# Graph layers on one core: three bias additions moved from VectorE to accumulating DMAs, a doubling moved to ScalarE

## The chip, the cores and the metric

The kernel runs on one core of a Trainium2 chip. TensorE (PE in the profile) multiplies matrices into PSUM, VectorE (DVE) and ScalarE (ACT) work on the 128 partitions of SBUF and PSUM, GpSimd (POOL) and SyncE (SP) here mostly issue DMAs. The metric is the time of one execution in microseconds of the device, as the median of several runs; smaller is better.

## The reference, cut to what matters

128 graphs of 64 nodes with 512 features each pass four layers, float32 throughout. Each layer ends in `x = layernorm(x + f(x))`.

```python
def _L0_gnn_ref(x, adj, W1, b1, gamma, beta, W2, b2):
    h = relu(hypergraph_conv(x, adj, W1, b1))
    h = layer_norm(h, gamma, beta)
    y = hypergraph_conv(h, adj, W2, b2)            # ... + b2
    return y + x
def _L1_gnn_ref(x, A_shape, w, a): ...             # attention over the adjacency, no bias
def _L2_gnn_ref(batch_graph, adj, W1, b1, W2, b2, W3, b3):
    x = relu(_gcn_layer(batch_graph, adj, W1, b1))
    x = relu(_gcn_layer(x, adj, W2, b2))
    return _gcn_layer(x, adj, W3, b3)              # ... + b3
def _L3_gnn_ref(x, mask, adjacency_mat, distance_mat, W_qkv, W_out, b_out):
    ...
    return out @ W_out + b_out

x = _layernorm(x + _L0_gnn_ref(x, ...))            # x + x + ... + b2: x is doubled
x = _layernorm(x + _L1_gnn_ref(x, ...))
x = _layernorm(x + _L2_gnn_ref(x, ...))            # ... + b3
x = _layernorm(x + _L3_gnn_ref(x, ...))            # ... + b_out
```

Three rows of 512 numbers are thus added to every node: `b2` in layer 0 (where `x` counts twice), `b3` in layer 2 and `b_out` in layer 3.

## The kernel before, in words

Two graphs fill the 128 partitions (a "pair"), four pairs make a group, and there are 16 groups. A group's `x` is one tile of 128 x 4 x 512 floats (1 MB), in one of three buffers; every layer works on it in place. A large product of a group (`multiply`, L546) is cut into seven smaller ones in the manner of Strassen and Winograd, named in `ORDER`: B11, T1, T2, B21, T3, B22, T4. Each is one call of `product` (L528) and eight 128x256 matmuls for a 512x512 weight (sixteen for `w2`). They share three PSUM accumulators: `pa` takes B11, T2, T3 and T4, `pc` T1 and B22, `pb` B21. Between them the accumulators are read out: after B11, T1 and T2 by `snap` (L555), after T3 by VectorE's addition at L589, after B22 by the one at L598, after T4 by L608 or L610. A product that accumulates on in `pa` cannot begin before the read of `pa` ahead of it is over.

The left-hand operand comes from `graph_T` (L470), which multiplies a group's `x` by a graph matrix, transposed, into four PSUM tiles (two for each "duo" of pairs); ScalarE copies them to SBUF (L492). VectorE then forms the sums S1 to S4 of its quarters (`Left.sums`, L514, lines L518 to L521).

Three groups are in work at a time: `a`, in layers 0 and 1 (`first_half`); `b`, in layer 2 and the front of layer 3 (`second_half`); `t`, the rest of layer 3 of the group before that. The string `order` (L1440) lists the pieces of one step, and TensorE executes them in this order. A step begins `t.v1 a.c1 t.v b.gt ...`: products B11, T1, T2 of `v` for group `t`, then `graph_T` of layer 0 for group `a`, then the other four products of `v`, then `graph_T` of layer 2 for group `b`. In the middle steps a scheduler decides, from a cost model, the order of the instructions on the other engines; `behind(key)` only asks that an instruction stands behind a named one of its own engine.

The places of the change:

- `doubled` (L890), called in `first_half` at L789 for groups 2 to 15: VectorE forms `2 x + b2`, four instructions of 128x512, in L892. Groups 0 and 1 are doubled in the written-out start, L1515. The next to touch this `x` is `constant` (L896, line L898), VectorE as well.
- `shifted` (L745), called in `second_half` (for the middle groups at L1142): VectorE adds `gb3_bc`, four instructions at L749. The next to touch this `x` is the addition at L1172.
- the addition of `bo_bc` at L1201, one VectorE instruction of 128x2048. The next to touch this `x` is the product with `Wout` (L1233), which adds `x` at L555.

GpSimd's DMA queue carries loads of rows and columns at the start, and the stores of the sums of weights that are formed once (L280), the last of them before 361 us. After that it is empty. SyncE's queue carries the loads of weights, in the order of use, into a ring of 20 buffers of 256 KB (`wring`; L236 and L238), the loads of `x` (L153) and the stores of the result (L1243).

Of the kernel before, what the change touches and what calls it, by code (L numbers as in the profile page):

```python
# [11 lines left out]
ALU = mybir.AluOpType  # L12
AX = mybir.AxisListType

P = 128
C = 64
D = 512
DH = 1024
HEADS = 8
G = 4  # L20
# [21 lines left out]
def kernel(  # L42
# [28 lines left out]
    nc = tc.nc  # L71
    NT = x.shape[0]
    NPAIR = NT // P
    NGRP = NPAIR // G
# [56 lines left out]
    ten, vec, act = Engine(nc.tensor, PE), Engine(nc.vector, DVE), Engine(nc.scalar, ACT)  # L131
# [61 lines left out]
    def load_row(src, n, name):  # L193
        t = const.tile([P, n], FP, name=name)
        nc.gpsimd.dma_start(out=t, in_=src.partition_broadcast(P))
        return t
# [244 lines left out]
    def row2(t, c0):  # L441

        return t[:, c0 : c0 + Q].unsqueeze(1).to_broadcast([P, 2, Q])
# [57 lines left out]
    def behind(key):  # L501
        return tc.issue_after(last_add[key]) if key in last_add else nullcontext()
# [222 lines left out]
    def prepare_masks(g):  # L725
        q = g["q"]
        mj, mr = g["mj"], g["mr"]

        neg = grp.tile([P, 2, 2, C], FP, name=f"neg_{q}", tag="neg", bufs=1)
        n3 = neg.rearrange("p a g j -> p (a g) j")  # L730
        vec.tensor_mul(
            n3, mj.rearrange("p a g j -> p (a g) j"), bcast(mi[:, q * G : (q + 1) * G], G)
        )
        vec.tensor_scalar(neg, neg, BIG, BIG, ALU.mult, ALU.subtract)

        m2 = grp.tile([P, G, C], FP, name=f"m2_{q}", tag="m2", bufs=1)
        vec.tensor_mul(m2, mr, bcast(mcol[:, q * G : (q + 1) * G], G))
        adt = g["adt"]
        if LD != LA:
            vec.tensor_scalar_mul(adt, adt, LD / LA)  # L740
        vec.scalar_tensor_tensor(adt, g["atc"], LG / LA, adt, ALU.mult, ALU.add)
        vec.tensor_mul(adt, adt, m2)
        g["neg"] = neg

    def shifted(g, key):  # L745

        with behind(key):
            for p in range(G):
                vec.tensor_add(g["x"][:, p, :], g["x"][:, p, :], gb3_bc)  # L749
            prepare_masks(g)  # L750


    def first_half(g):
        q, xg = g["q"], g["x"]
# [8 lines left out]
        for n in range(2):  # L763
            for i, _ in enumerate(multiply(
                [left], (w_1[n], q),
                lambda m, k: h[m][:, :, n * D + k * Q : n * D + (k + 1) * Q],
                f"l0w1{n}_{q}",
                res=lambda m, k: row2(b1_bc, n * D + k * Q),
                stops=((2, 4), (2, 3))[n] if q == 1 else (3,),
            )):  # L770
                yield f"w1{'ab'[n]}{i + 1}"
            yield "w1" + "ab"[n]

            if n == 0:
                st = small.tile([P, G, 2, 6], FP, name=f"sth_{q}", tag="sth", bufs=2)
            with behind(f"l0w1{n}_{q}"):
                for m in range(2):
                    hn = h[m][:, :, n * D : (n + 1) * D]
                    if n == 1 and m == 1:

                        act.activation(hn[:, :, Q:], hn[:, :, Q:], AF.Relu)
                        hn = hn[:, :, :Q]
                    act.activation(hn, hn, AF.Relu)  # L783
                    for p in range(2):
                        vec.bn_stats(st[:, 2 * m + p, n, :], h[m][:, p, n * D : (n + 1) * D])
            if n == 0:
                if q > 1:
                    with behind(f"l0w10_{q}"):
                        doubled(g)  # L789
                yield "resid"  # L790
        for m in range(2):
            mv = small.tile([P, 2, 2], FP, name=f"mvh_{q}_{m}", tag="mvh")
# [97 lines left out]
    def doubled(g):  # L890
        for p in range(G):
            vec.scalar_tensor_tensor(  # L892
                g["x"][:, p, :], g["x"][:, p, :], 2.0, b2_bc, ALU.mult, ALU.add
            )
# [184 lines left out]
    def second_half(g):  # L1079
        q, xg = g["q"], g["x"]  # L1080
# [34 lines left out]
        if q == 0:  # L1115
            shifted(g, f"l2b_{q}")
# [24 lines left out]
        if not alone:  # L1141
            shifted(g, f"l0w2_{q + 1}.u2")  # L1142
        h2.sums()
        if q == NGRP - 1:
            last_add["h2s"] = newest(DVE)
            shifted(g, "h2s")
# [51 lines left out]
        for _ in multiply([left], (w_q, q), turned(qT), f"q_{q}", flipped=True, stops=(5,)):  # L1198
            yield "q1"
        with behind(f"q_{q}"):  # L1200
            vec.tensor_add(xg, xg, bo_bc.unsqueeze(1).to_broadcast([P, G, D]))  # L1201
        yield "q"
        kT = big.tile([P, KD, T], FP, name=f"kT_{q}", tag="big")
        for _ in multiply([left], (w_k, q), turned(kT), f"k_{q}", flipped=True):
# [295 lines left out]
    for n, (who, q, name) in enumerate(todo):  # L1500
# [28 lines left out]
        elif who == "rest":  # L1529
            with in_turn(SP, POOL):  # L1530
                wa_parts = load_wa()
                b2_bc = load_row(b2, D, "b2_bc")
# [6 lines left out]
                gb3_bc = load_row(gb3, D, "gb3_bc")  # L1539
                bo_bc = load_row(bout, D, "bo_bc")  # L1540
# [70 lines left out]
```

## Time and profile before

| | |
|---|---|
| median of 3 runs | 2734.22 us (2732.8 to 2735.39) |
| span of the profiled execution | 2732.1 us, granted TensorE clock 1.000 |
| PE busy | 2714.7 us, 99% of the span |
| DVE busy | 2077.8 us, 76% |
| ACT busy | 803.9 us, 29% |
| POOL busy | 38.0 us, 1%, all of it before 361 us |
| DMA moved | 405.14 MB, mean 148 GB/s |
| L892, `x<-x,b_bc` | 56 instructions, mean 691 ns |
| L749, `x<-x,gb_bc` | 64 instructions, mean 685 ns |
| L1201, `x<-x,bo_bc` | 16 instructions, mean 2287 ns |

The profile was taken in one execution, whose span stands 2.1 us under the median. A row of the timeline reads: start in us from the beginning of the span, duration in us, engine, line, operation, what it writes and reads, shape, how many instructions were merged in the row, and in brackets how long the engine sat idle before it and what ended the wait. Instructions of an engine overlap: a 128x512 addition on DVE takes 0.69 us, while the next one begins 0.60 us after it. Row L127 stands for all operations that the recording helper `Engine` issues in the written-out start and end.

### The profile page before, as it was taken

How to read it: one execution, taken by the hardware profiler on the slowest of the kernel's cores; microseconds unless marked ns; L12 is line 12 of the kernel's file. 1: busy time of each engine (PE TensorE's matmuls, PEld its weight loads, DVE VectorE, ACT ScalarE, POOL GpSimd, SP SyncE). 2: the span in 40 equal slices, each digit the busy share in tenths (PEclk: the TensorE clock that was granted, in tenths of full speed). 3: DMA queues.
4: the chain of work that ended last, by engine and by line, in shares of the span. 5: the costliest groups of instructions: out<-in, count | busy, mean ns of one | idle time of the engine just before them, and what ended most of it. 6: DMA issues, size and time to landing. Idle time of an engine off the chain costs nothing.

```text
span 2732.1 us, 67726 instructions
## 1 busy us (share of the span) xinstructions
PE 2714.7 (99%) x28770; PEld 2347.7 (86%) x28770; DVE 2077.8 (76%) x4111; ACT 803.9 (29%) x1440; POOL 38.0 (1%) x71
## 2 busy tenths in 40 slices
PE   9999999999999999999999999999999999999998
PEld 7888888888888888888888888888888888888887
DVE  6878687876877778777786877778677687776766
ACT  3323223232232332323223233232322323233232
POOL 2000000000000000000000000000000000000000
PEclk9999999999999999999999999999999999999999
DMA  7545454454544545455454554545545455454541
GB/s 257 179 129 154 123 175 140 142 162 131 173 131 139 168 129 170 130 145 168 134 165 129 146 165 133 164 129 151 163 130 167 130 154 157 128 166 129 158 125 63
DMA packets 309532, 405.14 MB, mean 148 GB/s; under 512 B 57424, under 2 KB 185456, under 8 KB 309232
## 3 DMA queue, kind: packets, MB, share of 16 engines
q1 hardware_dynamic: 304256, 385.45, 48.2%
q0 software_dynamic: 4832, 15.24, 1.5%
q8 instruction: 228, 3.74, 0.6%
q14 instruction: 72, 0.59, 0.1%
q10 hardware_dynamic: 144, 0.13, 0.0%
HBM read 369.78 MB, written 30.93 MB: 147 GB/s over the span
## 4 chain that ended last, share of the span: by engine, by line
PE 96%; DVE 3%; ACT 1%; issue 0%; DMA 0%; DVEq 0%
PE a_l0w L539 15%; PE b_l0w L539 7%; PE a_l2b L539 4%; PE a_q L539 4%; PE a_k L539 4%; PE a_l2a L539 4%; PE a_v L539 4%; PE c_l0w L539 4%; PE a_l1w L539 4%; PE a_wo L539 4%; PE a_l2c L539 4%; PE gt_l L481 3%; PE gt_l0h L481 2%; PE b_l2a L539 2%; PE b_l1w L539 2%; PE b_l2b L539 2%
## 5 line engine op out<-in xcount | busy, mean ns | idle before, releaser
L539 PE MATMUL a_l0w<-w2w,aT_l0h 128*128 128x256 f32 x720 | 164.3, 381 | 0.0
L457 DVE BATCH_NORM_STATS2 st_l<-x 128x6 f32<-128x512 f32 x244 | 157.9, 676 | 0.6
L539 PEld LDWEIGHTS a_l0w<-w2w,aT_l0h 128*128 128x128 f32 x720 | 135.6, 190 | 18.8
L463 DVE TENSOR_SCALAR x<-x,mv_l,rs_l 128x512 f32<-128x512 f32 x244 | 119.3, 543 | 2.2
L539 PE MATMUL b_l0w<-w2w,s_l0h 128*128 128x256 f32 x480 | 108.5, 379 | 0.0
L783 ACT ACTIVATE h<-h 128x1024 f32<-128x1024 f32 (+1 forms) x58 | 55.0, 948 | 178.5 <-DVE h L598 157.4
L539 PEld LDWEIGHTS b_l0w<-w2w,s_l0h 128*128 128x128 f32 x480 | 91.1, 190 | 12.5
L1140 ACT ACTIVATE aT_h<-gth,gb_col 128x256 f32<-128x256 f32 x124 | 47.2, 491 | 159.0 <-PE gth L1128 159.0
L447 ACT ACTIVATE rs_l<-mv_l,eps_t 128x4 f32<-128x4 f32 (+1 forms) x63 | 18.8, 298 | 252.3 <-DVE mv_l L458 245.0
L492 ACT COPY aT_l<-gt_l 128x512 f32<-128x512 f32 x148 | 78.1, 597 | 46.4 <-PE gt_l L481 46.4
L555 DVE TENSOR_TENSOR u_l0w<-a_l0w,b_bc 128x512 f32<-128x512 f32 x56 | 38.6, 689 | 69.2 <-PE a_l0w L539 69.2
L539 PE MATMUL a_l2b<-gwbw,aT_h 128*128 128x256 f32 x360 | 86.6, 383 | 0.0
L539 PE MATMUL a_l2c<-gwcw,aT_h 128*128 128x256 f32 x360 | 86.3, 382 | 0.0
L539 PE MATMUL a_q<-aT_xT,wqw 128*128 128x256 f32 x360 | 85.1, 379 | 0.5 <-ACT aT_xT L1194 0.5
L539 PE MATMUL a_l1w<-ww,aT_l 128*128 128x256 f32 x360 | 85.1, 379 | 0.2 <-ACT aT_l L492 0.2
L539 PE MATMUL a_l2a<-aT_l,gwaw 128*128 128x256 f32 x360 | 85.0, 379 | 0.0
L539 PE MATMUL a_k<-aT_xT,wkw 128*128 128x256 f32 x360 | 85.0, 379 | 0.0
L539 PE MATMUL a_v<-wvw,aT_xT 128*128 128x256 f32 x336 | 81.1, 384 | 0.5 <-issue 0.5
L539 PE MATMUL a_l0w<-w1aw,aT_l 128*128 128x256 f32 x336 | 80.8, 383 | 0.0
L539 PE MATMUL a_wo<-wow,aT_oT 128*128 128x256 f32 x336 | 79.5, 379 | 0.0
L539 PE MATMUL a_l0w<-w1bw,aT_l 128*128 128x256 f32 x336 | 79.4, 379 | 0.0
L539 PEld LDWEIGHTS a_l2c<-gwcw,aT_h 128*128 128x128 f32 x360 | 67.2, 190 | 11.6 <-ACT u_l2c L555 3.0
(532 smaller groups left out, 6489.0 us busy)
## 6 DMA issues: line engine op xcount, KB each, us to landing
w2w<-w2k SPq DMA_DIRECT2D x210, 256.0 KB, 2.7
x<-in_x_dram SPq DMA_DIRECT2D x15, 1024.0 KB, 5.8
w1aw<-w1ak SPq DMA_DIRECT2D x60, 256.0 KB, 2.7
w1bw<-w1bk SPq DMA_DIRECT2D x60, 256.0 KB, 2.8
ww<-wk SPq DMA_DIRECT2D x60, 256.0 KB, 2.7
gwaw<-gwak SPq DMA_DIRECT2D x60, 256.0 KB, 3.4
gwbw<-gwbk SPq DMA_DIRECT2D x60, 256.0 KB, 2.7
gwcw<-gwck SPq DMA_DIRECT2D x60, 256.0 KB, 2.7
```

The source lines that it names most:

```text
L447: act.activation(rs[:, at], mv[:, at, 1], AF.Sqrt, bias=eps_t)
L457: vec.bn_stats(st, xg[:, p, :])
L463: vec.tensor_scalar(xg[:, p, :], xg[:, p, :], mv[:, p, 0:1], rs[:, p : p + 1], ALU.subtract, ALU.mult)
L481: ten.matmul(ps[g][f * C : (f + 1) * C, c, p, :], src(2 * duo + p)[rows, c0 : c0 + C], mat[rows, 2 * duo + p, :], start=True, stop=True,)
L492: act.copy(o[:, :, :, g, :], ps[g])
L539: ten.matmul(acc[:, blk, :], lhsT, rhs, start=(first and blk == 0 and i == 0), stop=(last and i == n_k - 1), skip_group_check=True,)
L555: last_add[f"{key}.{what}"] = (act.copy(t, ps) if res is None else vec.tensor_add(t, ps, res(m, n))).ins
L783: act.activation(hn, hn, AF.Relu)
L1140: act.activation(o[:, :, h, :], cols, AF.Relu, bias=gb2_col[:, k : k + 1])
```

## The change

A function `add_rows` issues one DMA on GpSimd's queue that adds a row of 512 floats, repeated over partitions and pairs, to a whole `x` tile of 1 MB in SBUF, by accumulation. It takes the place of VectorE's additions of `gb3_bc` and `bo_bc` in groups 1 to 14. In `first_half`, for groups 2 to 15, ScalarE multiplies the four pairs of `x` by 2.0, and `add_rows` adds `b2_bc`. Groups 0, 1 and 15 keep the old way where the diff says so. In all 42 DMAs and 56 multiplications are added, and 56 instructions of L892, 56 of L749 and 14 of L1201 are removed.

```diff
+    def add_rows(xg, row):
+
+        nc.gpsimd.dma_start(out=xg, in_=row.unsqueeze(1).to_broadcast([P, G, D]), accum_op=ALU.add)
+
     def shifted(g, key):
 
         with behind(key):
-            for p in range(G):
-                vec.tensor_add(g["x"][:, p, :], g["x"][:, p, :], gb3_bc)
+            if 0 < g["q"] < NGRP - 1:
+                add_rows(g["x"], gb3_bc)
+            else:
+                for p in range(G):
+                    vec.tensor_add(g["x"][:, p, :], g["x"][:, p, :], gb3_bc)
             prepare_masks(g)
...
             if n == 0:
                 if q > 1:
                     with behind(f"l0w10_{q}"):
-                        doubled(g)
+                        for p in range(G):
+                            act.mul(xg[:, p, :], xg[:, p, :], 2.0)
+                        add_rows(xg, b2_bc)
                 yield "resid"
...
         with behind(f"q_{q}"):
-            vec.tensor_add(xg, xg, bo_bc.unsqueeze(1).to_broadcast([P, G, D]))
+            if 0 < q < NGRP - 1:
+                add_rows(xg, bo_bc)
+            else:
+                vec.tensor_add(xg, xg, bo_bc.unsqueeze(1).to_broadcast([P, G, D]))
         yield "q"
```

The compiled program of the changed kernel has the same instructions in the same order on TensorE. On ScalarE the multiplications stand, in each of the 14 steps, where `graph_T` of layer 0 is copied out; at the same place VectorE's order differs too. Line numbers are those of the kernel before, "new" marks the added instructions.

```
ScalarE before              ScalarE after               VectorE before        VectorE after
L555 u_v<-a_v               L555 u_v<-a_v               L518 S1<-aT_l         L518 S1<-aT_l
L492 aT_l<-gt_l             new  x<-x (pair 0)          L519 S2               L568 v<-c_v,u_v
L492 aT_l<-gt_l             L492 aT_l<-gt_l             L520 S3               L519 S2
L492 aT_l<-gt_l             L492 aT_l<-gt_l             L521 S4               L520 S3
L492 aT_l<-gt_l             new  x<-x (pair 1)          L568 v<-c_v,u_v       L521 S4
L608 v<-a_v                 new  x<-x (pair 2)          L589 v<-a_v,u_v       L589 v<-a_v,u_v
                            L492 aT_l<-gt_l             L598 v<-b_v,u_v       L598 v<-b_v,u_v
                            L492 aT_l<-gt_l
                            new  x<-x (pair 3)
                            L608 v<-a_v
```

Two more exchanges recur in each step on ScalarE: the exponential of the last softmax quarter (L1337) moves ahead of the second `relu` of L783, and the square root for layer 3's normalization (L447) moves from behind two of the copies `u_k<-a_k`, `u_k<-b_k` (L555) to ahead of both. The number of ScalarE's table loads stays the same. On GpSimd's queue a step issues the DMA of `b2` for group `a`, then of `gb3` and of `bo` for group `b`.

## The prediction

> **What bounds the kernel now.** I read the page's busy times first, then the chain of waits by engine, then busy time by stretches of one step each, which decide.
>
> ```profile
> PE 2714.7 (99%) x28770; PEld 2347.7 (86%) x28770; DVE 2077.8 (76%) x4111; ACT 803.9 (29%) x1440; POOL 38.0 (1%) x71
> ...
> PE 96%; DVE 3%; ACT 1%; issue 0%; DMA 0%; DVEq 0%
> ```
>
> ```profile
> 1155.69:1323.67 167.98, 167.98 (x1793) 145.53 (x1793) 128.78 (x254) 49.37 (x89) 0.00 (x0) 1.00 0.51 148
> 1323.67:1491.63 167.96, 167.96 (x1793) 145.59 (x1793) 128.79 (x254) 49.36 (x89) 0.00 (x0) 1.00 0.50 148
> ...
> 1827.57:1996.97 169.40, 168.13 (x1794) 145.59 (x1793) 128.87 (x254) 49.57 (x89) 0.00 (x0) 1.00 0.51 147
> 1996.97:2164.94 167.97, 167.97 (x1793) 145.59 (x1793) 128.78 (x254) 49.37 (x89) 0.00 (x0) 1.00 0.51 148
> ```
>
> Each row is a step, cut at the first `w2` matmul of two groups in succession: length, then busy time of PE, PEld, DVE, ACT and POOL, the granted clock, the DMA engines' share, GB/s. A step takes 167.96 to 167.98 us and PE is busy for all of it, at clock 1.00. The one longer step holds a pause of 1.27 us that ended with "issue", in which PE waited for nothing that the profile names. So steps run at the pace of back-to-back matmuls (216 ns from one to the next). PE's idle time in the whole span is 2732.1 - 2714.7 = 17.4 us, of which 9.6 us are pauses before 202 us or behind 2638 us, outside the 14 changed steps. DVE is idle for 39 us of a step: nothing that is taken from DVE shortens a step, and any wait that PE is given lengthens it in full.
>
> **The change part by part.** Taken from DVE: 56 x 0.691 (L892) + 56 x 0.685 (L749) + 14 x 2.287 (L1201) = 38.7 + 38.4 + 32.0 = 109.1 us. It all lies beside a full PE: worth 0. It would be worth something only where PE waited for DVE, and in the 14 steps the trace has one such wait, of 0.27 us at 358 us.
>
> Added to ACT: 56 multiplications of 128x512. ACT is busy for 49 of 168 us, so the sum (56 x 0.54 = 30 us) is harmless; the place is not. Three of the four stand ahead of copies that DVE waits for. This is the place in one step of the kernel before, on PE, ACT and DVE:
>
> ```profile
> 1424.05 2.09 PE L481 MATMUL gt_l<-smat,x 64*64 64x64 f32 x128
> 1426.07 1.99 PE L539 MATMUL c_v<-wvw,aT_xT 128*128 128x256 f32 x8
> 1427.90 1.89 PE L539 MATMUL a_v<-wvw,aT_xT 128*128 128x256 f32 x8
> 1429.63 1.89 PE L539 MATMUL b_v<-wvw,s_xT 128*128 128x256 f32 x8
> 1431.36 1.89 PE L539 MATMUL a_v<-wvw,aT_xT 128*128 128x256 f32 x8
> ```
>
> ```profile
> 1423.66 0.63 ACT L1337 ACTIVATE sm<-sm 128x512 f32<-128x512 f32 x1
> 1424.21 0.59 ACT L555 COPY u_v<-a_v 128x512 f32<-128x512 f32 x1
> 1425.26 2.05 ACT L492 COPY aT_l<-gt_l 128x512 f32<-128x512 f32 x4 [0.46 <-PE gt_l L481]
> 1433.28 0.59 ACT L608 COPY v<-a_v 128x512 f32<-128x512 f32 x1 [5.97 <-PE a_v L539]
> ```
>
> ```profile
> 1427.34 0.69 DVE L518 TENSOR_TENSOR s_l<-aT_l 128x512 f32<-128x512 f32 x1 [0.82 <-ACT aT_l L492]
> ...
> 1430.48 0.68 DVE L589 TENSOR_TENSOR v<-a_v,u_v 128x512 f32<-128x512 f32 x1
> ```
>
> The fourth copy ends at 1425.26 + 2.05 = 1427.31, and S1 (L518) starts 0.03 us later. Behind it DVE runs S2 to S4, L568 and L589 and ends the latter at 1431.16. PE's last product of `v`, T4, starts at 1431.36 and accumulates in the `a_v` that L589 reads, so it may not start earlier than L589's end plus a signal; where PE did wait for DVE (195.87 to 195.93 us) that signal took 0.06. The slack is 1431.36 - 1431.16 - 0.06 = 0.14 us, the same within 0.07 in all 14 steps.
>
> In the changed order pair 0's multiplication comes first. It needs the matmuls of pair 0, the last of which stand 8 matmuls ahead of the duo's last (2.02 us for 128, so 0.12 us), so it starts at 1425.26 - 0.12 = 1425.14. The trace has no multiplication of this tile; the nearest row is the exponential, SBUF to SBUF in the same shape, which lasts 0.63 us and lets the next instruction start after 0.55 (1423.66 to 1424.21). Copies follow each other after 0.48. So: copies 1 and 2 at 1425.69 and 1426.17, multiplications at 1426.65 and 1427.20, copies 3 and 4 at 1427.75 and 1428.23, end at 1428.84 instead of 1427.31, which is 1.53 later. DVE starts S1 at 1428.87; L568, S2, S3, S4 and L589 follow at 0.60 each (L568 fills the 0.13 us that S2 waited for S1), so L589 starts at 1431.87, ends at 1432.55, and T4 starts at 1432.61 instead of 1431.36: **a wait of 1.25 us per step**. Bounds: at 0.48 for each multiplication (a copy's pace) 1.04; at 0.63 (no overlap) 1.49. I take 1.25, since the exponential differs only in its function. Behind T4 stand `graph_T` of layer 2 and the rest of the step; ACT's copy L608 and the copies of that `graph_T` wait for PE and move along by the same 1.25, as do DVE's softmax pieces, so nothing else is late. 14 x 1.25 = 17.5 us (14.6 to 20.9).
>
> The other exchanges on ACT cost 0, by their cover. The exponential ahead of the second `relu` (L783) is fed by DVE before L610, on which that `relu` waits (0.73 us idle before): it fits into that gap. The square root ahead of the `u_k` copies needs layer 3's statistics, which ended at 1408.18; with L1201's 2.2 us of issue gone they end near 1405.98, the copy starts at 1406.25 instead of 1405.94 and ends at 1406.84, and T2 of `k`, which needs it, starts at 1407.46. If that cover of 0.56 us were gone, every further tenth would cost 1.4 us in all.
>
> The 42 DMAs: an accumulating DMA is not in the trace. Nearest rows:
>
> ```profile
> x<-in_x_dram SPq DMA_DIRECT2D x15, 1024.0 KB, 5.8
> ...
> w2k<-w2t POOLq DMA_DIRECT2D x8, 256.0 KB, 7.7
> ```
>
> From below: the load of the same 1 MB, 5.8 us. From above: GpSimd's slowest row, four times its bytes, 31 us. Reading the destination too speaks for more than 5.8; I take 12. The cover is longer. `b2` can be issued when ACT has finished pair 3 (1429.4 us) and is first needed by L898 at 1488.53: 59 us. `gb3` can go after layer 2's `graph_T` (1435.3) and is needed by L1172 one step on, at 1538.6: 103 us. `bo` can go at about 1390 and is needed by L555's `u_wo<-a_wo,x` at 1531.7: 142 us. GpSimd's queue runs them in this order and holds nothing else in 13 of the 14 steps; there is no one to be late behind them. Cost 0. If `b2` took over 59 us, DVE would stop at L898 with the sums for `w2` behind it, and PE behind those.
>
> They share the DMA engines with weights. `gwaw`'s seven loads of one group are issued from 1407.7 to 1420.7 us, land within 6.2, and are used from 1447.4 to 1457.8: the last lands 30.9 us before its use. Engines are busy for 0.51 of a step; three MB at the load's pace add 3 x 5.8 / 168 = 0.10. A load that waits behind a whole 12 us DMA is still on time. Cost 0 at 12, some us per DMA only near 31.
>
> GpSimd's issue beside DVE: when it issued at 44.50 us, two normalizations (TENSOR_SCALAR) took 1.62 us, the first 0.91 where the row of L797 has 0.81; additions beside issues kept 0.68 to 0.69. At 1429.4 DVE runs additions: 0. The Trainium skill's "SBUF — State Buffer" (Who interferes with whom) speaks against the change: DVE instructions in a two-port mode lock GpSimd out while it writes descriptors, and the other way round. By that rule the DMA would start late by one DVE instruction; the sum would stay the same, for 59 us cover it.
>
> Sum: 2732.1 + 17.5 = 2749.6 us of span. The median stands 2.1 above the profiled span, so the forecast for the median is **2752 us**, 0.64% slower.
>
> **The rivals.** *Not slower: the multiplications fit into ACT's gap.* Place: the 0.46 us of idle ahead of L492. It decides if three multiplications delay the fourth copy by no more than 0.14 + 0.14 us (slack, and the S2 gap), so at most 0.28 in place of 1.53. For it: ACT is 29% busy. Against it: the multiplications of pairs 0 and 2 depend on the same matmuls as the copies, so the gap can't hold them, and none would last over 0.1 us. Time: 2734. *Faster through DVE.* Even if the steps over 167.97 (168.64, 169.21 and 169.40 us) lost their excess, 0.67 + 1.24 + 1.43 = 3.3 us, the time would be 2731, inside what counts as no change; more would need PE to run faster than back to back. *The DMAs are long.* At 31 us of full engines, weights with 30.9 us of lead would come late by a weight's own landing, 3 us: 42 x 3 = 126, so 2860 with nothing else; at half that pace nothing. For it: an unmeasured kind of DMA. Against: 31 us is four times a queue's slowest row. A smaller form, a few more "issue" pauses of 1.3 us since instructions are fetched by DMA too, gives 2755 to 2765.
>
> **How the numbers follow.** Forecast 0.76, its own range 2748 to 2757 (14 x 1.04 to 14 x 1.49, with 1 us for the runs' scatter). Not slower 0.12; faster by DVE 0.03; DMAs in either form 0.09. The range 2746 to 2764 takes the forecast, the smaller DMA form and a little of a partly hidden wait. A measurement tells about 0.2%, 5.5 us, from no change: faster 0.03, within 0.13, slower 0.84.
>
> **What would show it.** After the change, a step from `w2` to `w2` should be 169.2 us, with PE idle 1.25 us ahead of T4 of `v`, released by DVE's L589, 14 times, and DVE's S1 waiting for ACT's L492 1.5 us longer. DVE's busy time should fall by about 109 us, ACT's rise by about 30, with no PE wait anywhere else and weights landing over 20 us ahead. The prediction is wrong if steps stay at 167.97, or if DVE waits at L898, L1172 or L555 for a DMA.

## The result, and the profile after

The changed kernel takes 2762.56 us (median of 4 runs, 2761.29 to 2764.2) against 2734.77 us in the runs beside it: a ratio of 1.0105, 95% interval 1.0093 to 1.0118. It is slower by 28 us. The profiled execution has a span of 2759.5 us, 27.4 us longer than that of before.

First the page of the changed kernel: busy times, the DMA queues (packets, MB, share of 16 engines' time) and the chain of waits.

```profile
PE 2719.5 (99%) x28770; PEld 2346.8 (85%) x28770; DVE 1977.4 (72%) x3985; ACT 833.2 (30%) x1496; POOL 92.0 (3%) x113
...
q0 software_dynamic: 27008, 59.28, 11.3%
q8 instruction: 228, 3.74, 0.5%
...
PE 92%; DVE 5%; ACT 2%; issue 1%; POOL 0%; DVEq 0%; POOLq 0%
```

DVE's busy time fell by 100.4 us, ACT's rose by 29.3, POOL's by 54.0. PE's busy time rose by 4.8 us only, so most of the longer span, 22.6 us of 27.4, is new idle time of PE. The chain shows DVE with 5% instead of 3%, and "issue" with 1% instead of 0%.

Then busy time by stretches of one step, columns as before (length, PE, PEld, DVE, ACT, POOL, clock, DMA share, GB/s), and the waits of PE by what ended them (us in total, times, longest).

```profile
1338.08:1507.34 169.26, 168.24 (x1798) 145.56 (x1793) 121.61 (x245) 51.56 (x93) 3.87 (x3) 1.00 0.59 166
1507.34:1678.52 171.18, 168.39 (x1797) 145.54 (x1792) 121.61 (x245) 51.47 (x93) 3.84 (x3) 1.00 0.58 164
...
2186.30:2358.47 172.17, 168.40 (x1798) 145.56 (x1792) 121.61 (x245) 51.48 (x93) 3.87 (x3) 1.00 0.59 163
```

```profile
PE a_v L539 <- DVE v L589: 13.1, 13, 1.0
PE a_l0w L539 <- issue: 6.2, 3, 2.7
...
PE a_v L539 <- issue: 2.5, 1, 2.5
PE b_l0w L539 <- issue: 1.5, 1, 1.5
PE c_v L539 <- issue: 1.2, 1, 1.2
```

Two things are new. A plain step is 169.26 us instead of 167.97, and in each PE waits once for DVE's L589 (13 times in the list: in the 14th step a pause just ahead took the wait's place). And some steps are longer still, by pauses that end with "issue". Set step against step, the 27.4 us are:

| | us |
|---|---|
| 14 steps, each 1.29 longer, wait for L589 | 18.1 |
| four pauses behind `graph_T` of layer 2, in every fourth step (1.72 + 1.83 + 1.93 + 2.91 over 1.29) | 8.4 |
| other pauses, less those that before had | 1.2 |
| the start, ahead of the first step | -0.3 |

**The wait.** The place shown of before, now in the changed kernel: ACT, DVE and PE around ScalarE's copies of layer 0's `graph_T`. L797 on ACT is the multiplication by 2.

```profile
1439.64 0.63 ACT L797 ACTIVATE x<-x 128x512 f32<-128x512 f32 x1
1440.18 1.05 ACT L492 COPY aT_l<-gt_l 128x512 f32<-128x512 f32 x2
1441.12 1.16 ACT L797 ACTIVATE x<-x 128x512 f32<-128x512 f32 x2
1442.17 1.07 ACT L492 COPY aT_l<-gt_l 128x512 f32<-128x512 f32 x2
```

```profile
1443.28 0.69 DVE L518 TENSOR_TENSOR s_l<-aT_l 128x512 f32<-128x512 f32 x1 [2.27 <-ACT aT_l L492]
...
1446.29 0.68 DVE L589 TENSOR_TENSOR v<-a_v,u_v 128x512 f32<-128x512 f32 x1
```

```profile
1444.11 1.89 PE L539 MATMUL b_v<-wvw,s_xT 128*128 128x256 f32 x8
1447.02 1.99 PE L539 MATMUL a_v<-wvw,aT_xT 128*128 128x256 f32 x8 [1.02 <-DVE v L589]
```

From B21's `c_v` product (in the rows `c_v` is the accumulator `pb`, and `b_v` is `pc`), whose row lies 14.48 us further on here, S1 starts at 1443.28 - 14.48 = 1428.80 on the time axis of before, L589 at 1431.81 and T4 at 1432.54. T4 started at 1431.36 before. DVE's idle time ahead of S1 grew from 0.82 to 2.27 us. T4 thus starts 1.18 us late; the other 0.11 us of a step's 1.29 lie behind its first matmul, after which the second starts 0.32 us later instead of 0.22. The bracket of 1.02 us is shorter, since it is counted from the modelled end of the matmul before (0.38 us long, where the next one starts after 0.22).

**The pauses.** This is one of them, in PE's timeline, and GpSimd's issues around it:

```profile
2297.18 2.10 PE L481 MATMUL gt_l<-atc,x 64*64 64x64 f32 x128
2299.20 0.92 PE L539 MATMUL a_l0w<-w1aw,aT_l 128*128 128x256 f32 x3
2302.86 1.24 PE L539 MATMUL a_l0w<-w1aw,aT_l 128*128 128x256 f32 x5 [2.75 <-issue]
```

```profile
2292.29 1.29 POOL L747 DMA_DIRECT2D x<-b_bc  x1 [39.08 <-DVE s_l L518]
2299.62 1.28 POOL L747 DMA_DIRECT2D x<-gb_bc  x1 [6.04 <-PE gt_l L481]
```

PE stops in the middle of a product whose first matmuls have run, so it can hardly lack an operand or the accumulator. What it lacks is instructions. They come by DMA, in 228 packets of 16 KB on queue q8. The trace has 58,531 instructions of PE in the kernel before and 58,559 in the changed one (28,770 matmuls, as many weight loads, and those of its sequencer), 257 for each packet. Counting them in order of time shows what the pauses wait for: in the fourteen profiles of this case, 37 pauses of over 0.15 us end with "issue" behind the first 202 us. Each of them begins after 193 + 256 n instructions, where n is the number of packets that have landed when PE goes on, and PE goes on 0.8 to 1.6 us after the last of these landed.

The four steps from 929 to 1601 us of before hold 57 such packets, 14.25 for a step, which is why a place in the step meets the same packet in every fourth step. The packet of this place starts, from the first matmul of layer 2's `graph_T`, in steps 1, 5, 9 and 13:

| kernel | start of the packet, us | `b2`'s DMA, us |
|---|---|---|
| before | -0.89, -0.16, -0.91, -0.28 | none |
| after | 3.14, 3.11, 2.94, 3.40 | from -4.9 to 5.8 (step 1) |
| the ninth of the kernels below | -0.40, -0.43, -0.39, -0.01 | from 24.7 to 35.4 (step 1) |

The packets take 0.9 to 1.6 us. In the changed kernel they start 3 to 4 us later, and PE resumes 1.2 to 1.4 us after their end. `b2`'s DMA fills the time ahead of them: between 2292 and 2303 us the queues took (packets, MB, share of 16 engines)

```profile
q0 software_dynamic: 648, 1.29, 70.6%
q1 hardware_dynamic: 817, 1.03, 28.0%
q8 instruction: 1, 0.02, 0.5%
```

### The profile page after: what moved, and what is told of

It reads as the page before. It is cut to its first block, busy times and chain, and to the rows that moved or that the text cites. A ratio compares the mean times of both kernels' runs of the same rounds, so it can differ in the third digit from the quotient of the medians.

```text
span 2759.5 us, 67854 instructions
## 1 busy us (share of the span) xinstructions
PE 2719.5 (99%) x28770; PEld 2346.8 (85%) x28770; DVE 1977.4 (72%) x3985; ACT 833.2 (30%) x1496; POOL 92.0 (3%) x113
## 4 chain that ended last, share of the span: by engine, by line
PE 92%; DVE 5%; ACT 2%; issue 1%; POOL 0%; DVEq 0%; POOLq 0%
PE a_l0w L539 15%; PE b_l0w L539 7%; PE a_l2b L539 4%; PE a_q L539 4%; PE a_k L539 4%; PE a_l2a L539 4%; PE c_l0w L539 4%; PE a_l1w L539 4%; PE a_wo L539 4%; PE a_l2c L539 4%; PE a_v L539 3%; PE gt_l L481 3%; PE gt_l0h L481 2%; PE b_l2a L539 2%; PE b_l1w L539 2%; PE b_q L539 2%
## 5 line engine op out<-in xcount | busy, mean ns | idle before, releaser
L447 ACT ACTIVATE rs_l<-mv_l,eps_t 128x4 f32<-128x4 f32 (+1 forms) x63 | 18.7, 297 | 269.3 <-DVE mv_l L458 262.0
L555 DVE TENSOR_TENSOR u_l0w<-a_l0w,b_bc 128x512 f32<-128x512 f32 x56 | 38.5, 688 | 75.9 <-PE a_l0w L539 75.9
L539 PEld LDWEIGHTS a_v<-wvw,aT_xT 128*128 128x128 f32 x336 | 61.5, 190 | 28.5 <-DVE v L589 16.9
```

Of the source, the lines that this page charges most:

```text
L447: act.activation(rs[:, at], mv[:, at, 1], AF.Sqrt, bias=eps_t)
L539: ten.matmul(acc[:, blk, :], lhsT, rhs, start=(first and blk == 0 and i == 0), stop=(last and i == n_k - 1), skip_group_check=True,)
L555: last_add[f"{key}.{what}"] = (act.copy(t, ps) if res is None else vec.tensor_add(t, ps, res(m, n))).ins
```

## The experiments

All times are medians beside runs of the kernel before on the same chip. Ratios are to that kernel, with 95% intervals.

**1. The multiplications, or the DMAs?** Four kernels separate them. In the first, doubling and `b2` go back to VectorE; the DMAs of `gb3` and `bo` stay.

```diff
-                        for p in range(G):
-                            act.mul(xg[:, p, :], xg[:, p, :], 2.0)
-                        add_rows(xg, b2_bc)
+                        doubled(g)
```

> VectorE does the doubling and b2 again; gb3 and bo stay accumulating DMAs (28 in place of 42). Theory A (the change's loss is 14 waits of 1.29 us ahead of T4 of v, made by ScalarE's multiplications ahead of the copies of graph_T, 18 us, plus some 9 us of pauses ended by 'issue' beside the DMAs): the waits for L589 are gone, the pauses stay, time 2738 to 2744. Rival B (all of the loss, 28 us, comes from the DMAs' traffic, the wait for L589 being part of it): two thirds of it stays, 2753. Rival C (all of it comes from ScalarE's multiplications): 2735.

Measured: 2740.03 us (10 runs), ratio 1.0019 (1.0010 to 1.0029). No wait for L589; steps without a pause are 167.97 us again. Some 6 us remain:

```profile
PE a_v L539 <- issue: 5.5, 3, 1.9
```

They lie at another place than those above, about 15 us ahead of layer 2's `graph_T`, in steps 3, 7 and 11. The kernel before has such pauses as well, of 0.47 and 1.27 us in steps 3 and 11. They are not the whole cost: behind the pauses of steps 3 and 7 (1.91 and 1.92 us) the granted clock was 0.50 for 3.41 us each.

In the second, ScalarE multiplies where the change put it, and all three additions are VectorE's: no accumulating DMA.

```diff
                         for p in range(G):
                             act.mul(xg[:, p, :], xg[:, p, :], 2.0)
-                        add_rows(xg, b2_bc)
+                        for p in range(G):
+                            vec.tensor_add(xg[:, p, :], xg[:, p, :], b2_bc)
```

> ScalarE doubles x in the same place as in the changed kernel, VectorE does all three additions, no accumulating DMA. Theory A: 14 waits of 1.29 us for L589 stay, pauses ended by 'issue' fall back to the 2 us of before: 2752 to 2755. Rival B (DMAs make all of it): 2735. Rival C (multiplications make all of it): 2762.

Measured: 2750.95 us (4 runs), ratio 1.0059 (1.0042 to 1.0076). The wait is there in all 14 steps, without any DMA of the change, and no pause behind layer 2's `graph_T`:

```profile
PE a_v L539 <- DVE v L589: 14.1, 14, 1.0
...
PE a_v L539 <- issue: 1.4, 1, 1.4
PE b_v L539 <- issue: 1.2, 1, 1.2
```

In the third, the whole change is kept, all 42 DMAs and 56 multiplications, but the multiplications stand behind ScalarE's copy `u_l2a` of layer 2, which also starts `b2`'s DMA 27 us later.

```diff
+                yield "resid"
                 if q > 1:
-                    with behind(f"l0w10_{q}"):
+                    with behind(f"l2a_{q - 1}.u2"):
                         for p in range(G):
                             act.mul(xg[:, p, :], xg[:, p, :], 2.0)
                         add_rows(xg, b2_bc)
-                yield "resid"
```

> The changed kernel with the four multiplications put on ScalarE behind the copy u_l2a (u2), where it sat idle for some 5 us, instead of ahead of the copies of graph_T; all 42 DMAs stay, b2's starts some 27 us later. Theory A: no wait for L589, step 167.97 us but for pauses of some 9 us in all: 2738 to 2744. Rival B: 2760, as the changed kernel. Rival C: 2735.

Measured: 2733.79 us (10 runs), ratio 1.0001 (0.9992 to 1.0011). The steps, columns as above:

```profile
1161.12:1329.09 167.97, 167.97 (x1799) 145.59 (x1793) 121.86 (x245) 51.49 (x93) 3.84 (x3) 1.00 0.60 167
1329.09:1497.06 167.97, 167.97 (x1799) 145.59 (x1793) 121.87 (x245) 51.50 (x93) 3.87 (x3) 1.00 0.59 167
```

This is the same work as in the changed kernel, DMA share 0.60 included, at the pace of before. So neither ScalarE's work nor the DMAs' bytes cost anything that can be measured; their places do. It also shows what VectorE's relief is worth: its busy time is lower by 7 us per step, and the time is that of before. The profiled execution was the slowest of the ten (2738.62 us): in step 3 it has a pause of 3.23 us at the first kernel's place, and clock 0.50 for 6.83 us behind it.

The fourth is the third with `gb3`'s DMA delayed too, behind a copy of its row by VectorE that stands where the additions stood.

```diff
             if 0 < g["q"] < NGRP - 1:
-                add_rows(g["x"], gb3_bc)
+                row = work.tile([P, D], FP, name=f"gb3_{g['q']}", tag="w")
+                vec.tensor_copy(row, gb3_bc)
+                add_rows(g["x"], row)
```

> As e3_mul_late, and the DMA of gb3 waits for a VectorE copy of its row that stands where the additions stood, so it starts some 67 us later, among dense 128x256 products instead of directly behind graph_T of layer 2. If the pauses come from instruction fetches that run into an accumulating DMA just when short 64x64 matmuls use instructions fastest, they go: 2734 to 2737. If they come from the DMAs' traffic wherever it falls: as e3_mul_late, 2738 to 2744. If VectorE's relief were worth anything, this one would come in below 2730.

Measured: 2733.27 us (10 runs), ratio 0.9998 (0.9988 to 1.0007): as the third.

**2. Which DMA makes the pauses?** The third and fourth had moved the multiplications as well, so the pauses were tried with the multiplications in place. The fifth kernel is the changed one with that same delay for `gb3`'s DMA alone.

> The changed kernel with one thing moved: the DMA of gb3 waits for a VectorE copy of its row, so that it starts some 70 us later and no longer lies beside the DMA of b2. The multiplications and the DMA of b2 stay where the change put them. The wait for L589 of about 1.25 us per step is expected in every theory (18 us). Theory 'two accumulating DMAs side by side delay instruction fetches': the pauses ended by issue at +5.5 us behind graph_T of layer 2 in steps 1, 5, 9 and 13 are gone, time 2751 to 2753. Rival 'the DMA of b2 beside the fetch is enough': the pauses stay, 2757 to 2763. Rival 'the pauses come from the changed order on the engines, not from DMAs': they stay, 2757 to 2763.

Measured: 2760.06 us (4 runs), ratio 1.0095 (1.008 to 1.011). The theory of two DMAs side by side fell: with `gb3`'s DMA 68 us away, all four pauses are there, and the packets start at 2.79 to 2.99.

```profile
PE a_v L539 <- DVE v L589: 14.0, 14, 1.0
PE a_l0w L539 <- issue: 5.5, 3, 2.2
...
PE a_v L539 <- issue: 1.9, 1, 1.9
PE b_l0w L539 <- issue: 1.2, 1, 1.2
```

The sixth delays `b2`'s DMA instead, behind a copy of its row on VectorE.

```diff
                         for p in range(G):
                             act.mul(xg[:, p, :], xg[:, p, :], 2.0)
-                        add_rows(xg, b2_bc)
                 yield "resid"
+                if q > 1:
+                    with behind(f"l2a_{q - 1}.d"):
+                        row = work.tile([P, D], FP, name=f"b2_{q}", tag="w")
+                        vec.tensor_copy(row, b2_bc)
+                        add_rows(xg, row)
```

> The changed kernel with the other of the two DMAs moved: the DMA of b2 waits for a VectorE copy of its row behind the sums of layer 2, some 27 us later; the multiplications and the DMA of gb3 stay. The wait for L589 of about 1.25 us per step is expected in every theory (18 us). Theory 'two DMAs side by side': the pauses at +5.5 us are gone, 2751 to 2753. Rival 'the DMA of gb3 alone, which starts 2.4 us behind graph_T of layer 2 just ahead of the pauses, is enough': pauses stay, 2757 to 2763.

Measured: 2780.41 us (4 runs), ratio 1.0167 (1.015 to 1.0184), 17 us above the highest time that a theory gave. The pauses were gone, but PE had a new wait, and DVE in turn waited for the DMA:

```profile
PE a_l0w L539 <- DVE u_l0w L555: 21.3, 14, 2.1
```

```profile
DVE u_l0w L555 <- DMA x<-b: 48.2, 14, 4.0
```

`u_l0w` doesn't touch `x`. It comes from the same ring of seven `work` buffers as the copied row, and had to wait until the DMA had read the row from the buffer that it was to take. The ninth kernel gives the row a tile of its own and is otherwise the same.

```diff
-                        row = work.tile([P, D], FP, name=f"b2_{q}", tag="w")
+                        row = b2_row
```

> The run with b2's DMA late had a second edit hidden in it: the copied row stood in the ring of buffers that u_l0w also uses, and DVE waited there for the DMA that reads it (48.2 us in all, PE 21.3 us). Here the row has a tile of its own, all else as there: multiplications in place, b2's DMA some 27 us late, gb3's in place. Theory 'b2's DMA, where the change starts it, lies over an instruction fetch': the wait for L589 stays (18 us), no pauses at +5.5 us, 2751 to 2754. If the pauses at +5.5 us come back, the rival that names gb3's DMA: 2757 to 2763.

Measured: 2750.66 us (4 runs), ratio 1.0062 (1.0047 to 1.0077). That is as long as the second kernel (ratio 1.0059), which has no accumulating DMA. Waits of PE and two steps that were long in the changed kernel (its ninth and thirteenth):

```profile
PE a_v L539 <- DVE v L589: 13.8, 14, 1.0
...
PE a_v L539 <- issue: 1.0, 1, 1.0
```

```profile
1501.09:1670.35 169.26, 168.24 (x1797) 145.56 (x1793) 122.02 (x246) 51.47 (x93) 3.84 (x3) 1.00 0.59 166
2178.15:2347.42 169.27, 168.25 (x1799) 145.57 (x1793) 122.01 (x246) 51.48 (x93) 3.87 (x3) 1.00 0.60 166
```

These steps took 171.18 and 172.17 us in the changed kernel. The instruction packets start at -0.40, -0.43, -0.39 and -0.01, nearly as before the change. PE has 58,559 instructions in both kernels, so the packets' borders fall on the same places of the program, to one matmul. From the changed kernel to this one, `b2`'s DMA starts 30 us later and 11.9 us are gone.

The tenth was to show `b2`'s DMA alone: the kernel before, with `x + x` on VectorE and `b2` by DMA.

> The kernel before with only the addition of b2 made by DMA at the place of the change; VectorE doubles x (x + x) where it doubled and added. No work is put on ScalarE. Theory 'b2's DMA beside the fetch': no wait for L589, but pauses ended by issue 5 to 6 us behind graph_T of layer 2 in steps 1, 5, 9, 13, together 6 to 9 us: 2738 to 2743. Rival 'the pauses need the delay that ScalarE's multiplications bring as well': 2733 to 2735.

Measured: 2732.76 us (10 runs), ratio 0.9997 (0.9987 to 1.0006). It doesn't answer the question: VectorE's doubling stands later than ScalarE's, so the DMA started at 21.7 us instead of -4.9, as late as in the third kernel. That `b2`'s DMA at the change's place is enough by itself is therefore not shown; that the four pauses need it there is.

**3. Is it accumulation?** The kernel before, with a plain DMA that copies `x` onto itself behind the doubling.

```diff
                         doubled(g)
+                        nc.gpsimd.dma_start(out=xg, in_=xg)
```

> The kernel before, its additions on VectorE, and at the place of b2's DMA a plain DMA on GpSimd's queue that copies x onto itself (1 MB, no accumulation): traffic added, nothing saved. If accumulation matters, because it occupies the engines for longer: landing near 6 us and 2733 to 2736. If any megabyte there lies over the fetch: pauses at +5 to +6 us in steps 1, 5, 9, 13 and 2738 to 2743.

Measured: 2732.33 us (10 runs), ratio 0.9995 (0.9986 to 1.0005). It started at 21.8 us for the same reason, so it tells nothing of the pauses. It does give a price to compare: the same megabyte, from issue to landing (the last column, us), here and by the accumulating DMAs in the changed kernel.

```profile
x<-x POOLq DMA_DIRECT2D x14, 1024.0 KB, 5.3
```

```profile
x<-b_bc POOLq DMA_DIRECT2D x14, 1024.0 KB, 9.7
x<-gb_bc POOLq DMA_DIRECT2D x14, 1024.0 KB, 10.2
x<-bo_bc POOLq DMA_DIRECT2D x14, 1024.0 KB, 9.7
```

In the tenth kernel, where `b2`'s DMA starts at the same place as the plain one here, it took 10.0. The accumulating DMA also has another source, one row that is repeated, so that accumulation alone makes the difference is not shown.

**4. Where do the first kernel's 6 us come from?** `gb3` alone by DMA (the seventh kernel), and `bo` alone by DMA (the eighth), all else on VectorE:

> The kernel before with only the additions of gb3 made by DMA (14 DMAs); doubling and bo on VectorE. In the run with gb3 and bo by DMA the time was 6 us over that of before. If gb3's DMA caused them: about 2740. If bo's part (its DMA or the earlier normalization of layer 3 that it lets in) caused them: 2733 to 2735.

Measured: 2732.39 us (10 runs), ratio 0.9995 (0.9986 to 1.0004).

> The kernel before with only the addition of bo made by DMA (14 DMAs); doubling and gb3 on VectorE. If bo's part caused the 6 us of the run with gb3 and bo by DMA: about 2740, with pauses ended by issue some 15 us ahead of graph_T of layer 2. If gb3's DMA did: 2733 to 2735. If only both together do: 2733 to 2735 here and in the run with gb3 alone.

Measured: 2737.91 us (10 runs), ratio 1.0017 (1.0007 to 1.0026), with pauses of 1.65, 1.12 and 1.27 us in steps 3, 7 and 11 (before 0.47, none and 1.27). So it is `bo`'s part. Its DMA runs from -44 to -34 us and is long over at the pauses' place, -13. But without L1201 on VectorE the normalization ends earlier, and the store of the result and the load of `x` start 2 us earlier (in the median step at -24.7 and -19.0 us, before at -22.5 and -17.3). The last kernel leaves the addition of `bo` out in groups 1 to 14 (the outputs lack that row there) and has no DMA.

```diff
-            vec.tensor_add(xg, xg, bo_bc.unsqueeze(1).to_broadcast([P, G, D]))
+            if not 0 < q < NGRP - 1:
+                vec.tensor_add(xg, xg, bo_bc.unsqueeze(1).to_broadcast([P, G, D]))
```

> The kernel before with the addition of bo left out in groups 1 to 14, so that its outputs lack that row: layer 3's normalization, the load of x and the store of the result come 2.2 us earlier, as with bo's DMA, but there is no DMA. If that earlier place of load and store delays the fetch that lies 13 to 16 us ahead of graph_T of layer 2 (steps 3, 7, 11): 2737 to 2740 with 3 to 5 us of such pauses. If bo's DMA itself does: 2732 to 2735 without them.

Measured: 2739.37 us (10 runs), ratio 1.0019 (1.001 to 1.0029). Less work, no added DMA, and 6 us slower. The waits, and the stretches right behind the two longer pauses (columns as above; the clock is the third number from the end):

```profile
PE a_v L539 <- issue: 3.6, 2, 2.2
PE b_v L539 <- issue: 2.6, 1, 2.6
```

```profile
580.94:584.35 3.41, 3.41 (x8) 2.71 (x9) 0.44 (x1) 1.80 (x2) 0.00 (x0) 0.50 0.15 49
1932.62:1936.03 3.41, 3.41 (x10) 2.70 (x9) 1.31 (x3) 1.11 (x2) 0.00 (x0) 0.50 0.25 73
```

The pauses of steps 3, 7 and 11 are 6.2 us here and 1.7 before, and two stretches of 3.41 us at half clock cost some 3.4 us more (an estimate); the span of this profile is 7.4 us longer. So `bo`'s DMA is not needed for the loss. That the earlier store and load make it is argued from their place only, for no run moved them alone. And it stays open why the third and fourth kernels, whose store and load stand at the same early place, take the time of before: their profiles have 3.2 us of such pauses each.

## Why the prediction was right, and where it was short

The side, the range and the main mechanism held; the size was 28 us instead of 17.5, and most of the missing 10 us were a rival's. That the stated range, 2746 to 2764, holds 2762.56 is in part luck: it was drawn wide enough for that rival, and the sum itself had no term for it.

- *DVE's relief is worth 0.* Held. DVE's busy time fell by 100 us and not 109, because the removed 128x512 additions overlap (0.69 us each, 0.60 apart). The third, fourth, seventh and tenth kernels keep all or part of the relief and lie within 0.1% of before.
- *ScalarE's multiplications make T4 of `v` wait.* Held, step by step: S1 was put at 1428.87 and came at 1428.80, L589 at 1431.87 against 1431.81, T4 at 1432.61 against 1432.54, the first multiplication following the exponential's row to 0.01 us (0.63 long, the next instruction 0.54 later). T4 came 1.18 us late where 1.25 was forecast; with the 0.11 us behind its first matmul, which the forecast didn't have, a step lost 1.29, in all 18.1 us instead of 17.5. The second kernel shows this cost alone (17 us by the medians), and the third shows it gone with the place.
- *The other exchanges on ACT cost 0.* Held: no wait of PE that names them appears.
- *The DMAs land within their covers.* Held. They take 9.7 to 10.2 us where 12 was taken from bounds of 5.8 and 31 (the upper one was misread: GpSimd's slowest 256 KB row of before took 9.9 us, `w1bk<-w1bt`, not 7.7, so four times that is 40); DVE never waits for `x` in the changed kernel, and no wait of PE ends with a DMA.
- *"Cost 0 at 12" for the 42 DMAs.* This step failed. It asked who needs `x` and who needs weights next, both with covers of tens of us, and left out a third user of the DMA engines, PE's instructions, whose cover at the busiest place is short: against the ninth kernel `b2`'s DMA delayed their packet by 3.3 to 3.5 us once in every four steps and PE lost 1.7 to 2.9, so the cover was 0.5 to 1.8 us. That made 8.4 of the missing 10 us. The prediction had this as the "smaller form" of a rival, "a few more 'issue' pauses of 1.3 us", inside a chance of 0.09 for both forms, and its price of 2755 to 2765 holds the result, while the forecast's own range of 2748 to 2757 does not. It happened together with the forecast's wait, where the chances treated the two as alternatives.

The clue was on the page of before. Queue q8 is listed there with its 16 KB packets, and the one long step shown held a pause of 1.27 us ended by "issue". Why this place is tender can be read from PE's rows, though no run tested it: 128 matmuls of 64x64 with their weight loads are 256 instructions, a whole packet, and `graph_T` executes them in 2.1 us, where a product of eight 128x256 matmuls spreads 16 over 1.73 us. In `t.v1 a.c1 t.v b.gt` two such stretches stand close together, and around this place the packets of the kernel before follow each other after 5.8 to 7.4 us, where the mean is 168 / 14.25 = 11.8. The Trainium skill ("Runtime: NRT & Kernel Launch", Instruction fetch mechanics) says that instructions are refilled in blocks of 16 KB, 256 of them, by a DMA queue that the engine's sequencer drives, at a cost that is mostly hidden. The packets here agree (16 KB each, and the pauses begin only where a new 256 begin), and hidden they are in most steps; here the exception cost 1.7 to 2.9 us a time.

## What to carry to other kernels

Where one engine ran back to back, relief of the others was worth nothing, and instructions put ahead of something that it waits for were paid in full beyond the slack: look for the slack at the very place (here 0.14 us), not at busy shares. A large DMA that is early enough for its own user may still be in the way of others, and the engine's instructions are among them: the rows of PE suggest placing it away from stretches of many small matmuls, where instructions are used up fastest, though here only the one move of 30 us was tested. The change at its best place (the third kernel) is worth nothing here, and no version beat the kernel before.

## What the runs showed of the hardware that was not expected

- An accumulating DMA of 1 MB within SBUF took 8.7 to 10.7 us to landing (medians of the runs), a plain copy of the same tile onto itself 5.3: nearly twice the time. The Trainium skill ("DMA: Bandwidth & Descriptors", Anatomy of one DMA — SWDGE (gpsimd) path) gives a fit for GpSimd's DMAs from which 4.4 us would be estimated for 1 MB; the plain copy is nearer to it, and the accumulating one is not.
- GpSimd spent 1.28 us on each issue of such a DMA, 54 us in all, and DVE's additions beside it kept their 0.68 to 0.69 us.
- PE stopped at the first instruction of a packet of 256 that was late, and went on 0.8 to 1.6 us after its landing (37 pauses in fourteen profiles).
- Behind some pauses of 1.9 to 3.2 us the granted clock was 0.50 for 3.41 us (once 6.83) in the first, third, fifth, sixth and last kernels; in the changed kernel it stayed at 1.00 behind pauses of 2.45 and 2.75 us.
- Removing 32 us of VectorE's work (`bo` left out) made the kernel 6 us slower, without any added DMA.
